# Channel attention: products of channels by pairs of image columns on two column halves of TensorE, and strip-edge rows in 64x32 tiles with two edges at once

## The chip, the cores and the metric

The kernel runs on one core of one Trainium2 chip. The metric is the device time of one launch in microseconds (us), the median of several runs. The five engines of the core are called TensorE (PE; its weight loads PEld), VectorE (DVE), ScalarE (ACT), GpSimd (POOL) and SyncE (SP). SP and ACT also issue DMA transfers, each on its own queue (SPq, ACTq).

## The reference

Two layers on an input of 4 images, 192 channels and 128 by 128 pixels, in f32. The change touches the first, a channel attention with 8 heads of 24 channels:

```
qkv = dwconv3x3(conv1x1(x, w_qkv), w_dw)          # 768 channels
q, k, v, l = jnp.split(qkv, 4, axis=1)
q = q / jnp.maximum(jnp.linalg.norm(q, axis=-1, keepdims=True), EPS)   # over the 16384 pixels
k = k / jnp.maximum(jnp.linalg.norm(k, axis=-1, keepdims=True), EPS)
attn = jnp.einsum('bhcn,bhdn->bhcd', q, k) * temperature[None]         # 24 x 24 per head and image
attn = jax.nn.softmax(attn, axis=-1)
out = jnp.einsum('bhcd,bhdn->bhcn', attn, v).reshape(b, c, h, w)
...
out = conv1x1(L + out + x, w_proj) + L
```

L is a gate made from the mean of l. The second layer is a dilated local attention on the result. For the change it matters that each head needs, for every image, the 24 by 24 products of the convolved q and k channels over all pixels, and the squared norms of these channels.

## The kernel before, in words

The kernel has three parts in a row. The first pass (to about 845 us) makes the 1x1 products for q, k and v, convolves v, and writes q and k unconvolved into a DRAM buffer, `qk_dram`, ordered by image row, channel, image and column. `channel_attention` (about 845 to 1560 us) reads them back, convolves them on TensorE, and makes the attention weights and from these a mixing matrix for each image. The second pass (to the end) applies it and does the second layer. The first and last part have written-out plans; in `channel_attention` only the order of TensorE is that of the program text, and a scheduler places the instructions of the other engines, the DMA issues on SP and ACT among them.

A head is worked in two stages. In the **convolution**, `head` walks over its 48 channels (24 of q, then 24 of k). An image's 128 rows are cut into four strips of 32 rows, and a channel's four strips lie on the four groups of 32 partitions. `loaded` brings eight channels at a time: 16 transfers on SP's queue (L717) into one of three buffers (`lent`, and two called `u`), and one small transfer `few` (L703), from which POOL builds `band`, the matrices that apply the vertical taps (L728, L730). `convolve` (L738) multiplies with three of these, one for each horizontal tap, as 32 by 32 tiles: a strip sees only its own rows. `evicted` copies the sums from PSUM on ACT (L747) into one large tile for q and one for k, and VectorE takes the statistics for the norms (L749, `bn_stats`). These large tiles are ordered by image, group of four columns, channel and column in the group, so that four columns of all 24 channels are 96 adjacent numbers.

In the **products** (`products`), TensorE multiplies for each image and each group of four columns the 96 numbers of q with the 96 of k over the 128 rows (L838), and sums over the 32 groups into `gram`; of the result only the places with equal column count, which `kept` and `part` pick out at the end (L850, L856).

Rows at the inner edges of the strips are missing from this: for each of the three edges, two rows on either side. `cut_loaded` (L776) brings the four rows of the head's 24 channels, once for q and once for k, 96 partitions each; `cut_taps` (L766) brings the taps as a matrix. `cut_convolved` (L786) multiplies them, three taps by q and k, into `pcut`, q in the lower half of the partitions and k in the upper; ACT copies `pcut` to `s_cut` (L798), TensorE turns `s_cut` (L804) so that pixels lie on partitions, ACT copies that to `cutT` (L806), VectorE squares it and adds the squares to the norms (L811, L814). Small matmuls (L834) make the products of the edges, in the middle of the last image.

The order of TensorE in `products` is: for image 0, 1 and 2 the edge convolution of edge 0, 1 or 2, the 32 matmuls of the image, the turning of that edge; then image 3; then the folding of the sums (L858 to L866). Edge 0's rows are loaded by SP ahead of time, edges 1 and 2 by ACT's queue after the edge convolution that frees the buffers: there is one buffer for q and one for k. In images 0 and 1 the second half of the image's matmuls is preceded by the matmuls of the previous head's mixing matrix (`mix`, L906), with weights `wph` that were loaded once for all heads. The next head's rows (`lent`, `u`) are loaded by SP while the products run, as buffers come free. The softmax of a head (`finish`) and the gate are spread over the next head's convolution.

In the built program every DMA carries one of eight completion semaphores, taken in turn over both queues, and waits for the transfer that had this semaphore before it.

Of the kernel before, what the change touches and what calls it, by code (L numbers as in the profile page):

```python
# [670 lines left out]
def channel_attention(tc, d, load, qk_dram, mix1, mix2, band_p, u_p, gate_p, lent, gates):  # L671
# [7 lines left out]
    with ExitStack() as ctx:  # L679
# [11 lines left out]
        for band in bands:  # L691
            nc.gpsimd.memset(band, 0.0)
        logits = fin.tile([CH0, B, 2, CH0], F32, tag="logits", name="logits")
# [52 lines left out]
        def evicted(full, stats, ch, pc):  # L746
            nc.scalar.copy(full[:, :, :, ch, :], pc.rearrange("p b (v w) -> p b v w", w=4))  # L747
            for b in range(B):
                nc.vector.bn_stats(stats[:, b, ch, :], full[:, b, :, ch, :])  # L749
# [12 lines left out]
        def cut_taps(hd):  # L762
            both = []
            for which in range(2):
                t = cut_p.tile([4 * CH0, 3, 2 * CH0], F32, tag=f"taps{which}", name=f"cuttaps{which}_{hd}")
                nc.sync.dma_start(t, d["cuttaps"][:, which * HEADS0 + hd])  # L766
                both.append(t)
            return both

        def cut_loaded(hd, edge, queue):  # L770
            us = []
            for which in range(2):
                c0 = which * C + hd * CH0
                u = cut_p.tile([4 * CH0, B * W], F32, tag=f"u{which}", name=f"cut{which}_{hd}_{edge}")
                first = (edge + 1) * STRIP - 2
                queue.dma_start(u, qk_dram[first : first + 4, c0 : c0 + CH0].rearrange("r c b w -> r c (b w)"))  # L776
                us.append(u)
            return us

        def cut_convolved(hd, edge, us, taps):  # L780

            pcut = ps_c.tile([128, B, W], F32, tag="pc", name=f"pcut{hd}_{edge}")
            for dx in (1, 0, 2):
                to, of = shifted(dx)
                for which in range(2):
                    nc.tensor.matmul(  # L786
                        pcut[which * G : which * G + 2 * CH0, :, to],
                        taps[which][:, dx, :],
                        us[which].rearrange("p (b w) -> p b w", w=W)[:, :, of],
                        start=dx == 1,  # L790
                        stop=dx == 2,
                    )
            s_cut = cut_p.tile([128, B, W], F32, tag="s_cut", name=f"s_cut{hd}_{edge}")
            if hd == 0 and edge == 0:
                nc.gpsimd.memset(s_cut, 0.0)
            for which in range(2):
                rows = slice(which * G, which * G + 2 * CH0)
                nc.scalar.copy(s_cut[rows], pcut[rows])  # L798
            return s_cut

        def cut_turned(hd, edge, s_cut):
# [4 lines left out]
            nc.scalar.copy(cut, turned.rearrange("p b (k c) -> p b k c", k=2)[:, :, :, : 2 * CH0])  # L806
            return cut

        def cut_squares(hd, edge, cut, sums):
            square = st.tile([128, B, 2, 2 * CH0], F32, tag="square", name=f"square{hd}_{edge}")  # L810
            nc.vector.tensor_mul(square, cut, cut)  # L811
            for which, sq in enumerate(sums):
                for r in range(2):
                    nc.vector.tensor_add(sq, sq, square[:, :, which, r * CH0 : (r + 1) * CH0])  # L814

        def products(hd, q, sq, k, sk, us, taps):
            gram = ps_c.tile([128, B, W], F32, tag="pc", name=f"gram{hd}")[:HALF, :, :HALF]
            cuts, two = [], 2 * CH0
            for b in range(B):
                if b < 3:  # L820
                    s_cut = cut_convolved(hd, b, us, taps)
                    if b < 2:
                        us = cut_loaded(hd, b + 1, nc.scalar)
                for v in range(W // 4):
# [12 lines left out]
                    four = lambda a: a[:, b, v].rearrange("p c w -> p (c w)")  # L837
                    nc.tensor.matmul(gram[:, b, :], four(q), four(k), start=v == 0, stop=v == W // 4 - 1)  # L838
# [3 lines left out]

            own = st.tile([two, B, CH0], F32, tag="own", name=f"own{hd}")
            other = st.tile([two, B, CH0], F32, tag="other", name=f"other{hd}")
            for r, to in enumerate((own, other)):
                pick_row = same_row[:, r : r + 1].unsqueeze(1).to_broadcast([two, B, CH0])
                nc.vector.tensor_mul(to, extra[:, :, r * CH0 : (r + 1) * CH0], pick_row)
            nc.vector.tensor_add(own, own, other)
            kept = st.tile([128, B, CH0, 4], F32, tag="square", name=f"kept{hd}")[:HALF]
            nc.vector.tensor_mul(  # L850
                kept,
                gram.rearrange("p b (c w) -> p b c w", w=4),
                same.unsqueeze(1).unsqueeze(1).to_broadcast([HALF, B, CH0, 4]),
            )
            part = st.tile([HALF, B * CH0], F32, tag="part", name=f"part{hd}")
            nc.vector.reduce_sum(part, kept.rearrange("p b c w -> p (b c) w"), axis=AX.X)  # L856
# [17 lines left out]
        def finish(hd):  # L874
# [21 lines left out]
            mixes.append(mix(hd))  # L896

        def mix(hd):

            low = min(max(128 - hd * CH0, 0), CH0)  # L900
            for b in range(0, B, 2):
# [3 lines left out]
                for e in range(2):  # L905
                    nc.tensor.matmul(two[:, e, :], logits[:, b + e, hd % 2, :], wph[:, hd, :], start=True, stop=True)  # L906
# [18 lines left out]
        def head(hd):  # L925

            fulls, stats = [], []
            for which, pool in enumerate((q_p, k_p)):
                fulls.append(pool.tile([128, B, W // 4, CH0, 4], F32, tag="conv", name=f"conv{which}_{hd}"))
# [3 lines left out]
            for _, n, dx in order:  # L933
                which, j, e = n // CH0, n % CH0 // 4, n % 4
                if dx == 1:
                    if n % 8 == 0:
                        sources[n // 8] = loaded(hd, which, j)
                    if n == 40:
                        taps = cut_taps(hd)
                        us = cut_loaded(hd, 0, nc.sync)  # L940
# [12 lines left out]
        same, same_row, fold, fold_rows, ones, ident, wph, tempr = (  # L953
            load(wts, n) for n in "same same_row fold fold_rows ones ident wph temp".split()
# [517 lines left out]
def _shapes_only():  # L1472
# [4 lines left out]
    eye = np.eye(C, dtype=f).reshape(2, HALF, C).transpose(1, 0, 2)  # L1477
    pick = np.zeros((128, QR + 32), f)
# [123 lines left out]
```

## Time and profile before

| | us |
|---|---|
| median of 3 runs | 4336.97 (4332.42 to 4344.78) |
| the profiled execution, device time | 4341.44 |
| its span, first to last instruction | 4339.7 |
| TensorE busy over the span | 4154.4 (96%) |
| VectorE busy | 3816.2 (88%) |
| POOL busy | 3395.5 (78%) |
| ACT busy | 2633.3 (61%) |
| channel attention alone, 845 to 1560 us: TensorE busy | 673.8 of 715 |
| VectorE / ACT / POOL busy there | 419.6 / 285.3 / 206.0 |
| L838 gram, busy on TensorE | 192.6 |
| L786 edge convolution, busy on TensorE | 90.7, idle before it 28.0 |
| L738 convolution, busy on TensorE | 262.9 (rows from `u`), 140.0 (from `lent`) |

Busy time of TensorE is the union of its instructions, which overlap. A timeline line gives start, duration, engine, source line, operation, the tile written and the tiles read, the shape (stationary, then moving operand), the number of instructions merged, and in brackets the idle time before with what ended it. An f32 matmul stands as two records. A line of windows gives for each engine the busy time and the number of instructions, then the granted clock of TensorE as a share, the busy share of the DMA engines and the GB/s moved.

### The profile page before, as it was taken

The page shows a single profiled execution, that of the slowest core. Times are in us where ns is not written, and L with a number is a line of the kernel's source. Part 1 is how long each engine was busy: PE and PEld are TensorE (multiplying, and loading weights), DVE is VectorE, ACT ScalarE, POOL GpSimd, SP SyncE. Part 2 cuts the span into 40 slices and gives each one's busy share as a digit, 9 for nine tenths or more (in the row PEclk, how much of TensorE's full clock was granted, in tenths as well). Part 3 has the DMA queues.
Part 4 walks back from the last instruction along what each step waited for, and adds up shares of the span by engine and source line. Part 5 has one row for each costly group of instructions (what it writes and reads, how often), then busy time and mean ns, then how long its engine had stood idle before and what let it go on. Part 6 is the DMA issues. An engine that isn't in the chain of part 4 may idle for free.

```text
span 4339.7 us, 74888 instructions
## 1 busy us (share of the span) xinstructions
PE 4154.4 (96%) x25728; PEld 1722.2 (40%) x25728; DVE 3816.2 (88%) x5572; ACT 2633.3 (61%) x4906; POOL 3395.5 (78%) x3411
## 2 busy tenths in 40 slices
PE   8999999798999988999999999999999999999996
PEld 3333333376666632333333333333333333333331
DVE  6999999865566637999999999999999999999996
ACT  6999999743344456556566555665656556566531
POOL 6888888732233115999999999999999999999998
PEclk9999999899999999999999999999999999999997
DMA  7888898666556657566665566655556555655521
GB/s 236 265 267 256 266 287 279 202 184 171 162 148 178 169 123 138 122 133 124 135 131 128 131 121 133 136 119 131 125 132 133 129 130 124 136 133 126 115 51 32
DMA packets 483019, 676.93 MB, mean 156 GB/s; under 512 B 142848, under 2 KB 318412, under 8 KB 482640
## 3 DMA queue, kind: packets, MB, share of 16 engines
q1 hardware_dynamic: 440352, 498.53, 41.1%
q0 software_dynamic: 37888, 166.74, 20.9%
q10 hardware_dynamic: 4400, 6.88, 0.5%
q8 instruction: 204, 3.34, 0.3%
q14 instruction: 175, 1.43, 0.1%
HBM read 278.18 MB, written 201.33 MB: 110 GB/s over the span
## 4 chain that ended last, share of the span: by engine, by line
PE 72%; DVE 13%; DMA 4%; issue 4%; POOL 4%; ACT 1%; SPq 1%; POOLq 0%; DVEq 0%; ACTq 0%
PE sc L1260 9%; PE ex L1382 8%; PE ph L1027 7%; PE pu L427 7%; PE pc L738 6%; PE pkv L1181 5%; DVE term L1388 4%; PE pkv L1184 4%; PE pu L432 3%; PE q L1241 3%; PE gram L838 3%; PE q L1238 3%; POOL acc L1391 3%; DVE prod L1249 3%; PE pu L578 2%
## 5 line engine op out<-in xcount | busy, mean ns | idle before, releaser
L1391 POOL TENSOR_TENSOR acc<-acc,term 128x512 f32<-128x512 f32 x1536 | 2034.6, 1330 | 145.3 <-DVE term L1388 58.9
L1388 DVE TENSOR_TENSOR term<-ex,vring 128x512 f32<-128x512 f32 (+2 forms) x1596 | 1000.1, 663 | 56.1 <-PE ex L1382 42.6
L1249 DVE TENSOR_TENSOR prod<-q,kring 128x1536 f32<-128x1536 f32 (+1 forms) x600 | 1007.4, 1688 | 23.6 <-PE q L1238 9.0
L504 POOL TENSOR_TENSOR v_True<-v_True,side 128x512 f32<-128x512 f32 (+1 forms) x512 | 643.1, 1268 | 127.7 <-ACT side L493 98.4
L1382 PE MATMUL ex<-e_sb,spread 108*128 108x512 bf16 x1728 | 568.0, 387 | 55.6 <-DVE term L1388 31.8
L481 DVE SCALAR_TENSOR_TENSOR pa<-vboth,dwv,pa 128x1024 f32<-128x1024 f32 (+1 forms) x448 | 574.3, 1282 | 44.3 <-ACT pa L474 14.5
L1194 ACT COPY kring<-pkv 64x512 f32<-64x512 f32 x384 | 223.2, 581 | 416.0 <-PE pkv L1184 410.5
L1079 DVE SCALAR_TENSOR_TENSOR pa<-hboth,posw,pa 128x1024 f32<-128x1024 f32 (+1 forms) x320 | 408.3, 1276 | 35.9 <-ACT pa L1067 16.9
L1260 PE MATMUL sc<-prod,pick 128*32 128x512 f32 x3456 | 429.0, 598 | 1.8 <-DVE prod L1249 1.8
L728 POOL COPY band<-few 32x720 f32<-32x720 f32 x192 | 150.6, 784 | 335.9 <-DMA few<-in_bands 289.8
L1382 PEld LDWEIGHTS <-spread 108*128 108x128 bf16 x1728 | 133.3, 98 | 666.8 <-issue 640.9
L1407 ACT COPY o<-po 128x512 f32<-128x512 f32 x192 | 106.2, 588 | 447.2 <-PE po L1404 241.9
L427 PE MATMUL pu<-xt,wx 128*128 128x512 f32 x768 | 360.5, 613 | 17.1 <-ACT vboth L463 8.7
L1027 PE MATMUL ph<-lent,mix 128*64 128x512 f32 (+1 forms) x1024 | 373.7, 595 | 0.5 <-DMA mix<-mixed 0.5
L1181 PE MATMUL pkv<-y,wkv 128*128 128x512 f32 x768 | 364.3, 596 | 9.2 <-DMA y<-moved 9.0
L493 ACT ACTIVATE side<-ring,dwv 128x512 f32<-128x512 f32 (+1 forms) x512 | 347.9, 724 | 30.5 <-POOL v_True L504 26.5
L1111 ACT ACTIVATE side<-hring,posw 128x512 f32<-128x512 f32 (+1 forms) x512 | 340.9, 710 | 16.7 <-DMA side<-side 14.8
L749 DVE BATCH_NORM_STATS2 stats<-conv 128x6 f32<-128x128 f32 x1536 | 301.5, 271 | 17.0 <-ACT conv L747 15.3
L747 ACT COPY conv<-pc 128x512 f32<-128x512 f32 x384 | 219.1, 585 | 123.5 <-PE pc L738 116.4
L738 PE MATMUL pc<-u,band 32*32 32x508 f32 (+1 forms) x6144 | 262.9, 595 | 2.4 <-DMA u<-qk_dram 2.3
L1194 ACT COPY vring<-pkv 64x512 f32<-64x512 f32 x384 | 223.9, 583 | 45.6 <-PE pkv L1184 32.2
L427 PEld LDWEIGHTS pu<-xt,wx 128*128 128x128 f32 x768 | 143.6, 194 | 224.4 <-issue 124.2
(170 smaller groups left out, 6489.2 us busy)
## 6 DMA issues: line engine op xcount, KB each, us to landing
qk_dram<-us SPq DMA_DIRECT2D x192, 512.0 KB
side<-side POOLq DMA_DIRECT2D x124, 768.0 KB, 7.2
u<-qk_dram SPq DMA_DIRECT2D x512, 128.0 KB
xt<-in_x SPq DMA_DIRECT2D x64, 512.0 KB
v_dram<-v_False SPq DMA_DIRECT2D x64, 512.0 KB
lent<-qk_dram SPq DMA_DIRECT2D x256, 128.0 KB
lent<-in_x SPq DMA_DIRECT2D x128, 256.0 KB
lent<-v_dram SPq DMA_DIRECT2D x128, 256.0 KB
```

Source lines behind the costliest of these rows:

```text
L427: mm(pu, wx[:, mt * 128 : (mt + 1) * 128], tiles["xt", n][:, im, :], start=True, stop=False)
L481: nc.vector.scalar_tensor_tensor(by_row(to[:, o : o + length]), by_row(vboth[:, at : at + length, :, t % 3 : t % 3 + W]), dwv[:, 0, t : t ...
L504: nc.gpsimd.tensor_add(v[:, rows, :], v[:, rows, :], z[:, rows, :])
L738: nc.tensor.matmul(pc[r * STRIP : (r + 1) * STRIP, :, to], band[at, e, c, dx, :], u[at, e, c, :].rearrange("p (b w) -> p b w", w=W)[:, :, of],
L1027: mm(to, w[:, cols], tiles["xv", n, j, im], start=j == 0, stop=j == 2)
L1181: mm(rows3(tile_of("pc", key)), w, tiles["y", n, im], start=True, stop=False)
L1194: nc.scalar.copy(rows[HALVES[im], :, pad : pad + W], rows3(tiles["pkv", n, pair, im])[HALVES[e]])
L1249: nc.vector.tensor_mul(to[:, :, px].rearrange("p t (r w) -> p t r w", w=W), q.unsqueeze(1).to_broadcast([128, 3, *q.shape[1:]]), three,)
L1260: mm(sc[quad * 32 : (quad + 1) * 32, :], pick[:, QR - 4 * row : QR - 4 * row + 32], tiles["prod", n, k // NT, k % NT // 3][:, k % 3, :], s ...
L1382: mm(rows3(tile_of("ex", ("ex", n, g, t))), spread[:, t, :], e_sb, start=True, stop=True)
L1388: nc.vector.tensor_mul(rows3(to[:, px]), rows3(ex[:, px]), win)
L1391: nc.gpsimd.tensor_add(tiles["acc", n, g], tiles["acc", n, g], tiles.pop(("term", n, g, t)))
```

## The change

The large tiles of q and k are ordered by image, **pair** of columns, channel and column in the pair. For each image there are 64 pairs; a matmul takes 48 numbers of q and 48 of k, and successive pairs go to the lower and the upper half of the output partitions, that is, of TensorE's columns. `kept` and `part` are made for each half.

Edge rows: the 24 channels are split into two halves of 12. A half's four rows lie on 48 partitions of the lower or the upper 64, and q and k side by side in one buffer; so an edge has four transfers (L775 in the new text) instead of two, half as large. The taps come as one tile. `cut_convolved` takes a list of edges and multiplies in tiles of 64 rows by 32 columns; edges 0 and 1 are done together at the start of the products, on eight tiles, edge 2 alone at the end of image 0, on four. There are two buffers: edges 0 and 1 are loaded by SP with the head's last rows, edge 2 by ACT's queue after edges 0 and 1 are convolved. `cut_kept` is the copy to `s_cut`, now one instruction an edge. In odd edges the halves lie the other way round, which the copy to `cutT` undoes. The squares and the picking of rows follow the new order. `wph` is loaded for each head anew, on ACT's queue, when its softmax is done. The tables of constants (`same`, `same_row`, `fold`, `fold_rows`, `cuttaps`) are laid out to match.

```diff
-            nc.scalar.copy(full[:, :, :, ch, :], pc.rearrange("p b (v w) -> p b v w", w=4))
+            nc.scalar.copy(full[:, :, :, ch, :], pc.rearrange("p b (v w) -> p b v w", w=2))
...
         def cut_taps(hd):
+            taps = cut_p.tile([128, 2, 3, STRIP], F32, tag="taps", name=f"cuttaps{hd}")
+            nc.sync.dma_start(taps, d["cuttaps"][:, hd])
+            return taps
+
+        def cut_loaded(hd, edge, queue):
+            u = cut_p.tile([128, 2, B * W], F32, tag=f"u{edge % 2}", name=f"cut{hd}_{edge}")
+            first = (edge + 1) * STRIP - 2
             for which in range(2):
+                for h in range(2):
+                    c0 = which * C + hd * CH0 + h * (CH0 // 2)
+                    queue.dma_start(
+                        u[h * G : h * G + 2 * CH0, which],
+                        qk_dram[first : first + 4, c0 : c0 + CH0 // 2].rearrange("r c b w -> r c (b w)"),
+                    )
+            return u
+
+        def cut_convolved(hd, edges, us, taps):
+
+            pcut = {edge: ps_c.tile([128, B, W], F32, tag="pc", name=f"pcut{hd}_{edge}") for edge in edges}
             for dx in (1, 0, 2):
                 to, of = shifted(dx)
+                for edge in edges:
+                    for which in range(2):
+                        for h in range(2):
+                            rows = slice(h * G, h * G + 2 * CH0)
+                            at = (2 * which + (h + edge) % 2) * STRIP
+                            nc.tensor.matmul(
+                                pcut[edge][at : at + STRIP, :, to],
+                                taps[rows, which, dx, :],
+                                us[edge][rows, which].rearrange("p (b w) -> p b w", w=W)[:, :, of],
+                                start=dx == 1,
+                                stop=dx == 2,
+                            )
+            return pcut
+
+        def cut_kept(hd, edge, pcut):
             s_cut = cut_p.tile([128, B, W], F32, tag="s_cut", name=f"s_cut{hd}_{edge}")
-            if hd == 0 and edge == 0:
-                nc.gpsimd.memset(s_cut, 0.0)
-            for which in range(2):
-                rows = slice(which * G, which * G + 2 * CH0)
-                nc.scalar.copy(s_cut[rows], pcut[rows])
+            nc.scalar.copy(s_cut, pcut[edge])
             return s_cut
...
         def products(hd, q, sq, k, sk, us, taps):
-            gram = ps_c.tile([128, B, W], F32, tag="pc", name=f"gram{hd}")[:HALF, :, :HALF]
+            gram = ps_c.tile([128, B, W], F32, tag="pc", name=f"gram{hd}")[:, :, : 2 * CH0]
             cuts, two = [], 2 * CH0
+            pcut = cut_convolved(hd, (0, 1), us, taps)
+            us[2] = cut_loaded(hd, 2, nc.scalar)
+            s_cut = cut_kept(hd, 0, pcut)
             for b in range(B):
-                if b < 3:
-                    s_cut = cut_convolved(hd, b, us, taps)
-                    if b < 2:
-                        us = cut_loaded(hd, b + 1, nc.scalar)
...
-                    four = lambda a: a[:, b, v].rearrange("p c w -> p (c w)")
-                    nc.tensor.matmul(gram[:, b, :], four(q), four(k), start=v == 0, stop=v == W // 4 - 1)
+                    for e in range(2):
+                        pair = lambda a: a[:, b, 2 * v + e].rearrange("p c w -> p (c w)")
+                        nc.tensor.matmul(
+                            gram[e * G : e * G + two, b, :], pair(q), pair(k), start=v == 0, stop=v == W // 4 - 1
+                        )
                 if b < 3:
                     cuts.append(cut_turned(hd, b, s_cut))
                     cut_squares(hd, b, cuts[b], (sq, sk))
-
+                if b == 0:
+                    pcut.update(cut_convolved(hd, (2,), us, taps))
+                if b < 2:
+                    s_cut = cut_kept(hd, b + 1, pcut)
...
+            kept = st.tile([128, B, CH0, 2], F32, tag="kept", name=f"kept{hd}")
+            for e in range(2):
+                rows = slice(e * G, e * G + two)
+                nc.vector.tensor_mul(
+                    kept[rows],
+                    gram[rows].rearrange("p b (c w) -> p b c w", w=2),
+                    same[rows].unsqueeze(1).unsqueeze(1).to_broadcast([two, B, CH0, 2]),
+                )
+                nc.vector.reduce_sum(part[rows], kept[rows].rearrange("p b c w -> p (b c) w"), axis=AX.X)
...
         def mix(hd):

             low = min(max(128 - hd * CH0, 0), CH0)
+            wph = fin.tile([CH0, C], F32, tag="wph", name=f"wph{hd}")
+            nc.scalar.dma_start(wph, d["wph"][:, hd, :])
+            yield
...
-                fulls.append(pool.tile([128, B, W // 4, CH0, 4], F32, tag="conv", name=f"conv{which}_{hd}"))
+                fulls.append(pool.tile([128, B, W // 2, CH0, 2], F32, tag="conv", name=f"conv{which}_{hd}"))
...
                         taps = cut_taps(hd)
-                        us = cut_loaded(hd, 0, nc.sync)
+                        us = {edge: cut_loaded(hd, edge, nc.sync) for edge in range(2)}
```

## The prediction

> **What bounds the kernel now.** I read the page first, then the channel attention alone (845 to 1560 us) by waits, then each head cut into its convolution and its products, then one head's timeline by engine. The products of head 2 and of head 7, and the convolution before head 2's products, by windows:
>
> ```profile
> core 0: us, PE busy (x) PEld busy (x) DVE busy (x) ACT busy (x) POOL busy (x), PEclk, DMA share, GB/s
> 1066.30:1114.00 47.70, 42.53 (x359) 30.53 (x364) 11.89 (x39) 7.14 (x12) 13.01 (x36) 0.86 0.53 142
> ...
> 1510.20:1547.60 37.40, 37.21 (x354) 28.83 (x353) 10.70 (x39) 7.13 (x12) 0.00 (x0) 1.00 0.08 25
> ```
>
> ```profile
> 1024.60:1066.30 41.70, 41.66 (x1154) 30.38 (x1154) 40.44 (x201) 28.40 (x51) 13.94 (x36) 1.00 0.73 192
> ```
>
> In the products TensorE carries the time and all else is idle; in the convolution VectorE is busy for 40.4 of 41.7 us, so that stage yields nothing to a faster TensorE. The eight product stretches are 37.6, 46.9, 47.7, 45.6, 46.3, 46.3, 44.1 and 37.4 us (351.9). Heads 1 to 6 take some 9 us more than 0 and 7; TensorE's timeline in head 2 shows where:
>
> ```profile
> 1066.26 2.77 PE L786 MATMUL pcut<-cut,cuttaps 96*48 96x512 f32 x12
> ...
> 1072.60 2.96 PE L838 MATMUL gram<-conv,conv 128*96 128x96 f32 x32
> ...
> 1078.27 1.91 PE L786 MATMUL pcut<-cut,cuttaps 96*48 96x512 f32 x2 [2.28 <-DMA cut<-qk_dram]
> 1082.31 5.33 PE L786 MATMUL pcut<-cut,cuttaps 96*48 96x512 f32 x10 [2.12 <-DMA cut<-qk_dram]
> 1087.57 4.95 PE L838 MATMUL gram<-conv,conv 128*96 128x96 f32 x32
> ...
> 1099.23 5.68 PE L838 MATMUL gram<-conv,conv 128*96 128x96 f32 x64
> ...
> 1107.99 1.28 PE L834 MATMUL sm<-cutT 128*48 128x48 f32 x24
> ```
>
> Edge 1's rows come late, and what follows runs slow: ten edge records take 5.33 us where twelve took 2.77, and 32 gram records 4.95 instead of 2.96, with a granted clock of 0.86 in this stretch against 1.00 in head 7. A matmul has two records. The loads, in ScalarE's and SyncE's timelines of the same head and SyncE's waits over the stage:
>
> ```profile
> 1072.67 0.66 ACTq L776 DMA_DIRECT2D cut<-qk_dram  x1
> ```
>
> ```profile
> 1059.04 9.29 SPq L717 DMA_DIRECT2D lent<-qk_dram  x16
> ```
>
> ```profile
> SPq L717 <- DMA cut<-qk_dram: 75.7, 21, 7.1
> ```
>
> ScalarE issues edge 1's two loads at 1071.58 and 1072.67, 5.3 and 6.4 us after the products begin, and the second lands at 1082.3, 9.6 us after its issue. SyncE begins the next head's rows 7.2 us before the products. They share the DMA with the next head's rows, and in the built program each transfer also waits for the one that used its completion semaphore (of eight, in turn) before it, across both queues.
>
> **The change, part by part.** T is the start of a head's products. Times are against the profiled execution: span 4339.7, device 4341.4, which is 4.5 above the median of the runs.
>
> Gram. Before: 1024 matmuls of 96 by 96, 64 records an image, 5.68 us, so (5.68-0.25)/64 = 85 ns a record. After: twice as many of 48 by 48, alternating between two halves of the columns. A record of that shape stands in the trace in one half only (L834): (1.28-0.21)/24 = 45 ns. That the halves run beside each other is bounded by: 45 ns a record (no overlap) and 22.5 (full). The nearest rows are the edge records, two tiles of 64 columns over the same rows: twelve in 2.77 us, where one alone takes 0.59 and follows its own tile's last by 0.43, that is six rounds of two, full overlap. I take 24 ns: 3.1 us an image.
>
> [...]
>
> Edge convolution. Before: three edges of 2.77 us, each on two tiles. After: edges 0 and 1 together on eight tiles, 48 records in six rounds of 0.43: 2.8 us; edge 2 on four tiles, 24 records, also 2.8 at full clock. Two thirds of the old time. The convolution at L738 runs on 16 such diagonal tiles into one bank.
>
> Loads. Edges 0 and 1 now come on SP's queue behind the last group of the head's own rows: 7.2 us before T, where the next head's rows begin now, eight transfers and one for the taps instead of two and two. So edge 1's wait goes. **Late next are edge 2 and s_cut of edge 0.** Edge 2's four transfers are issued by ScalarE after pcut of edges 0 and 1, and s_cut's copy stands behind all four in ScalarE's order; turned of edge 0 on TensorE waits for that copy, and behind it edge 2's convolution and images 1 to 3. Before, the first of two issues fell 5.3 to 6.3 us after T. The semaphore that the first now needs belongs to a transfer four places earlier (2.3 us), but SP's queue runs some 4.5 us later (nine transfers at 0.3 to 0.65): T+8 for the first, T+11 for the fourth, whose semaphore belongs to the second transfer of the next group. s_cut is done at T+11.6, edge 2 (same bytes as edge 1 before, which took 8 to 11 us from first issue to last landing) at T+17.3. TensorE has done pcut and image 0 by 2.8+3.1+0.8 = 6.7. So it idles, and the clock falls as in head 2.
>
> One head of 1 to 6: 17.3, edge 2 at the slow clock 5.3, image 1 partly slow 4.1, pm 0.8, turned 0.5, image 2 3.1, turned 0.5, image 3 3.1, extra products 1.15, tail 1.9 (as now): 37.7 against 46.1 on average, 8.4 saved, 50 for six. Head 0: its first issue came 2.8 us after T with nothing ahead of it, the landing 10.7 after T; full clock: 10.7+2.8+3.1+0.5+3.1+0.5+3.1+1.15+1.9 = 27, saves 10.6. Head 7 has no next head's rows: landing T+8.7 (issues at 2.8 to 5.2 as head 7's were, and an estimate of 3.5 to land), 25.7, saves 11.7. Together 72.
>
> Taken off: the edges' rows land behind the last group, 0 to 1 us after the convolution's end; and the built order sends each group's bands (few) just before its rows, where some went earlier; POOL needs 4.7 us for a group's copies (4 of 784 ns, 8 of 196) and by my estimate of SP's queue has 2 us in hand. I take 1 us for each of seven heads, 7; the ends are 0 and 5 each (0 and 35).
>
> Everything else goes on covered engines. ScalarE: 24 s_cut copies fewer (0.58 each, 14 us) and one wph load a head; it is busy 7 of 47 us in the products. wph for the last head is placed by the built order in head 7's products, so its tail hides it; without that it costs one load, under 6 us (an edge load of head 7, issued at 1513.86, was in use at 1519.83). VectorE: kept and part in two halves instead of one, about 1.1 us either way, on the path in the tail. The sums at L814 and the reversed read at cutT keep size and count. SP's later next group delays nothing: it needs 62 us of queue a head (96 row transfers at 0.57, few, edges), the shorter period is 80.
>
> The convolution's copy now writes runs of two instead of four, and bn_stats reads them. ScalarE's 585 ns for runs of four equals 588 (L1407) for contiguous ones, and it has 13 us a head in hand. VectorE has none:
>
> ```profile
> L749 DVE BATCH_NORM_STATS2 stats<-conv 128x6 f32<-128x128 f32 x1536 | 301.5, 271 | 17.0 <-ACT conv L747 15.3
> ...
> L758 DVE TENSOR_TENSOR sq<-sq,stats 128x96 f32<-128x96 f32 x16 | 5.4, 336 | 0.6
> ...
> L757 DVE TENSOR_SCALAR sq<-sq 128x96 f32<-128x96 f32 x16 | 3.8, 240 | 0.6
> ```
>
> bn_stats is free of cost at one end, since runs of four leave it at 301.5/1536 = 196 ns for 128 elements. The other end is a read that hops at every element, (336-240)/96 = 1 ns an element, 128 ns an instruction, 197 us in all. A gain has no ground: the elements are as many. I take 0: a run of two is nearer to the run of four. [...] No row here has pairs.
>
> Sum: 4341.4 - 72 + 7 = 4276, at the median's level **4271**.
>
> **The rivals.** *The edge comes earlier*: if edge 2 lands at T+13, the gap is short enough for the clock to hold (head 0 kept it through 1.8 us), a head takes 13+2.8+14.15 = 30: 47 us more saved, 4224. For it: fewer of SP's transfers may stand ahead. Against: 8 to 11 us a load in every busy head. *The convolution loses*: 4 us a head from late bands or rows, 21 more than taken: 4292. VectorE's 95% speaks for it, the 2 us in hand against. *The halves don't overlap*: 45 ns a record adds 2.7 us to images 1 to 3, 8 a head, 65: 4336, no change. The edge records speak against it. *Slower*: VectorE's read of pairs costs. It decides at 66/1536 = 43 ns an instruction (a third of the hopping price), and at the full price gives 4468; the rest of the change can't pay it, since the convolution has no slack on VectorE. Against it: runs of four are free.
>
> **How the numbers follow.** Likeliest case 0.54 (own range 4240 to 4300: landing 3 us either way over six heads, the convolution's 0 to 3), earlier edge 0.10, convolution loses 0.14, halves don't overlap 0.10, slower 0.12. Faster by over 0.3% (13 us, about what a measurement of this kernel tells from none): the first three, 0.78; within: 0.10; slower: 0.12. The range 4215 to 4340 holds all but the last and the edge of the second.
>
> **What would show it.** Gram's busy time near 100 us instead of 192.6; edge records 5.6 us a head; TensorE in heads 1 to 6 waiting for s_cut some 5 us and for edge 2 some 5, with a clock below 1 in those stretches; product stretches near 38, 27 and 26 us; convolutions still 42 to 43 with VectorE at 40 and bn_stats at 196 ns. Wrong if bn_stats grows, if gram stays near 180 us, or if edge 2 lands after T+25.

## The result, and the profile after

The changed kernel takes 4292.48 us (median of 4 runs, 4289.94 to 4295.9), 0.9896 of the time before (95% interval 0.9878 to 0.9913): 45 us faster, where 66 were forecast. The profiled executions differ by more than the medians: span 4339.7 before, 4288.2 after, 51.5 less. Of these, 59.5 come from the products and 14.1 are lost in the convolutions of heads 1 to 7. The rest nearly cancels inside the channel attention (its chain of heads ends at 1501.2 us instead of 1547.6), and 5 us lie behind it.

The windows of the eight product stretches after the change, with the columns as before (busy time and number for each engine, then the granted clock, the DMA share, GB/s):

```profile
896.70:928.76 32.06, 29.28 (x643) 18.96 (x650) 11.79 (x39) 4.99 (x9) 12.92 (x36) 0.84 0.51 140
972.80:1015.39 42.59, 34.86 (x652) 19.88 (x657) 11.63 (x42) 5.27 (x9) 13.06 (x36) 0.80 0.57 157
1058.80:1101.91 43.11, 39.66 (x652) 23.75 (x657) 13.05 (x42) 5.27 (x9) 13.52 (x36) 0.72 0.58 159
1145.85:1182.13 36.28, 33.32 (x651) 19.94 (x657) 11.52 (x42) 5.23 (x9) 10.80 (x30) 0.86 0.59 167
1226.56:1262.23 35.67, 33.33 (x652) 20.64 (x657) 11.65 (x42) 5.26 (x9) 10.14 (x28) 0.81 0.60 165
1306.47:1341.17 34.70, 32.80 (x652) 20.59 (x657) 11.56 (x42) 5.27 (x9) 8.49 (x24) 0.80 0.56 156
1386.29:1417.47 31.18, 28.40 (x652) 17.88 (x656) 11.10 (x42) 5.28 (x9) 8.39 (x24) 1.00 0.52 149
1464.40:1501.22 36.82, 34.60 (x647) 21.08 (x645) 11.05 (x42) 5.26 (x9) 0.00 (x0) 0.81 0.30 79
```

Only head 6 has the clock at 1.00. In head 2 TensorE shows as busy for 39.66 of 43.11 us, but much of that runs at half speed (a granted clock of 0.50 from 1064.4 to 1074.7 us and from 1078.9 to 1087.0). Its timeline there (the last line is image 3's first half, at a granted clock of 1.00):

```profile
1058.80 1.43 PE L791 MATMUL pcut<-cut,cuttaps 48*32 48x512 f32 x10
1060.39 1.04 PE L791 MATMUL pcut<-cut,cuttaps 48*32 48x512 f32 x2 [0.16 <-DMA cut<-qk_dram]
1062.20 5.19 PE L791 MATMUL pcut<-cut,cuttaps 48*32 48x512 f32 x36 [0.77 <-DMA cut<-qk_dram]
1067.32 2.80 PE L847 MATMUL gram<-conv,conv 128*48 128x48 f32 x64
...
1078.89 5.30 PE L791 MATMUL pcut<-cut,cuttaps 48*32 48x512 f32 x18 [0.56 <-DMA cut<-qk_dram]
1084.12 2.80 PE L847 MATMUL gram<-conv,conv 128*48 128x48 f32 x64
...
1091.92 3.09 PE L847 MATMUL gram<-conv,conv 128*48 128x48 f32 x128
...
1095.52 1.64 PE L847 MATMUL gram<-conv,conv 128*48 128x48 f32 x64
```

Edges 0 and 1 (L791), 2.8 us of work (2.79 in head 0), last from 1058.80 to 1067.3, because their rows trickle in; the clock then falls (granted 1.00 up to 1064.4, 0.50 from there to 1074.7), and half an image takes 2.80 us where the last line has 1.64. What brought the rows, in SyncE's and ScalarE's timelines of the same head:

```profile
1051.08 5.14 SPq L775 DMA_DIRECT2D cut<-qk_dram  x8
1056.33 0.42 SPq L705 DMA_DIRECT2D few<-in_bands  x1
1056.85 12.12 SPq L719 DMA_DIRECT2D lent<-qk_dram  x16
```

```profile
1069.41 3.18 ACTq L775 DMA_DIRECT2D cut<-qk_dram  x4
1072.63 0.58 ACT L802 COPY s_cut<-pcut 128x512 f32<-128x512 f32 x1 [12.85 <-DMA few<-in_bands]
```

The eight edge transfers take 5.14 us to issue, up to 1056.22, 2.6 us before the stretch begins. TensorE's weight loads show the last wait for their rows:

```profile
1063.23 0.18 PEld L791 LDWEIGHTS pcut<-cut,cuttaps 48*32 48x32 f32 x16 [0.90 <-DMA cut<-qk_dram]
```

It ends 4.4 us into the stretch and seven us after the last issue. Edge 2's four issues follow 10.6 us after the start of the stretch, and s_cut's copy stands behind them.

The convolution: the windows of heads 1, 2 (the shortest) and 7 (the longest), then the two groups whose operands became runs of two columns (busy time, mean of one in ns, idle time before and what ended most of it), and ScalarE's copy as it was before:

```profile
928.76:972.80 44.04, 44.04 (x1152) 29.87 (x1153) 40.93 (x201) 29.71 (x51) 8.86 (x24) 1.00 0.66 176
1015.39:1058.80 43.41, 42.68 (x1152) 29.01 (x1152) 40.62 (x201) 29.57 (x51) 12.86 (x36) 1.00 0.66 179
...
1417.47:1464.40 46.93, 45.90 (x1154) 26.98 (x1153) 42.25 (x201) 29.22 (x51) 17.24 (x48) 1.00 0.80 208
```

```profile
L751 DVE BATCH_NORM_STATS2 stats<-conv 128x6 f32<-128x128 f32 x1536 | 304.4, 274 | 29.2 <-ACT conv L749 26.6
L749 ACT COPY conv<-pc 128x512 f32<-128x512 f32 x384 | 228.7, 616 | 127.6 <-PE pc L740 120.5
```

```profile
L747 ACT COPY conv<-pc 128x512 f32<-128x512 f32 x384 | 219.1, 585 | 123.5 <-PE pc L738 116.4 <-POOL band L730 3.3
```

VectorE is still the bound there (40.2 to 42.3 us busy over the seven heads), bn_stats rose from 271 to 274 ns, and its idle time behind ScalarE from 15.3 to 26.6 us. ScalarE's copy rose from 585 to 616 ns.

### The profile page after: what moved, and what is told of

It reads as the page before. It is cut to its first block, busy times and chain, and to the rows that moved or that the text cites. A ratio compares the mean times of both kernels' runs of the same rounds, so it can differ in the third digit from the quotient of the medians.

```text
span 4288.2 us, 79574 instructions
## 1 busy us (share of the span) xinstructions
PE 4115.1 (96%) x28064; PEld 1642.4 (38%) x28064; DVE 3820.6 (89%) x5588; ACT 2627.7 (61%) x4882; POOL 3388.9 (79%) x3411
## 4 chain that ended last, share of the span: by engine, by line
PE 68%; DVE 14%; DMA 5%; issue 4%; POOL 3%; SPq 3%; ACT 1%; ACTq 0%; POOLq 0%; DVEq 0%
PE sc L1281 9%; PE ex L1403 8%; PE ph L1048 7%; PE pu L427 6%; PE pkv L1202 5%; PE pc L740 5%; DVE term L1409 4%; PE pkv L1205 4%; PE q L1262 4%; PE q L1259 4%; PE pu L432 3%; DVE prod L1270 3%; PE gram L847 2%; POOL acc L1412 2%; SPq L719 2%
## 5 line engine op out<-in xcount | busy, mean ns | idle before, releaser
L481 DVE SCALAR_TENSOR_TENSOR pa<-vboth,dwv,pa 128x1024 f32<-128x1024 f32 (+1 forms) x448 | 574.2, 1282 | 42.2 <-ACT pa L474 14.4
L1100 DVE SCALAR_TENSOR_TENSOR pa<-hboth,posw,pa 128x1024 f32<-128x1024 f32 (+1 forms) x320 | 407.5, 1273 | 37.0 <-ACT pa L1088 18.1
L751 DVE BATCH_NORM_STATS2 stats<-conv 128x6 f32<-128x128 f32 x1536 | 304.4, 274 | 29.2 <-ACT conv L749 26.6
L749 ACT COPY conv<-pc 128x512 f32<-128x512 f32 x384 | 228.7, 616 | 127.6 <-PE pc L740 120.5
L740 PE MATMUL pc<-u,band 32*32 32x508 f32 (+1 forms) x6144 | 276.0, 595 | 4.1 <-DMA u<-qk_dram 1.9
```

The lines of the kernel that those rows point to most:

```text
L481: nc.vector.scalar_tensor_tensor(by_row(to[:, o : o + length]), by_row(vboth[:, at : at + length, :, t % 3 : t % 3 + W]), dwv[:, 0, t : t ...
L740: nc.tensor.matmul(pc[r * STRIP : (r + 1) * STRIP, :, to], band[at, e, c, dx, :], u[at, e, c, :].rearrange("p (b w) -> p b w", w=W)[:, :, of],
```

## The experiments

Every run stands beside runs of the kernel before on the same chip (medians 4334.8 to 4339.3). "Products" is the sum of the eight product stretches, "convolution" that of heads 1 to 7, both from the profiled execution; where a stretch ends can be read to some hundredths of a us, so the sums may be off by 0.2. Head 0's convolution is in neither sum: 54.0 us before, 55 to 56 in most runs, 60 to 64 in the five from "three buffers, ACT" to the last "one half". What follows the heads is the same program everywhere and took 2781 to 2798 us in these executions, so the time of one execution says little about differences below some 15 us; the medians and the two sums say more.

| kernel | us | ratio to before (95%) | products | convolution |
|---|---|---|---|---|
| before | 4337.36 | 1 | 352.0 | 297.8 |
| changed | 4292.48 | 0.9896 (0.9878 to 0.9913) | 292.5 | 311.9 |
| gram alone | 4319.32 | 0.9952 (0.9937 to 0.9967) | 329.3 | 305.2 |
| edges alone | 4327.15 | 0.9967 (0.9955 to 0.9980) | 333.9 | 308.8 |
| pairs in one half | 4327.15 | 0.9970 (0.9959 to 0.9981) | 334.7 | 304.1 |
| edges 0, 1 early | 4278.75 | 0.9854 (0.9825 to 0.9883) | 246.3 | 345.4 |
| three buffers, SP | 4251.67 | 0.9797 (0.9783 to 0.9812) | 194.8 | 374.2 |
| the same, later | 4271.46 | 0.9846 (0.9823 to 0.9868) | 193.7 | 393.2 |
| three buffers, ACT | 4244.56 | 0.9787 (0.9753 to 0.9821) | 246.9 | 306.2 |
| the same, fours | 4288.45 | 0.9875 (0.9854 to 0.9897) | 286.3 | 307.1 |
| ACT in written order | 4270.82 | 0.9843 (0.9826 to 0.9861) | 193.7 | 377.0 |
| the same, fours | 4342.55 | 1.0007 (0.9997 to 1.0017) | 270.5 | 372.5 |
| the same, one half | 4352.71 | 1.0029 (1.0017 to 1.0041) | 279.7 | 372.7 |
| an issue each third copy | 4275.95 | 0.9870 (0.9851 to 0.9889) | 202.3 | 378.5 |

The theory at the start: the gram and the edge records cost what was forecast, and what is missing went into late rows of edges 0 and 1 and into the convolution. The rivals: the halves overlap only in part, or the ScalarE chain (four issues, s_cut, edge 2) takes the time as forecast.

### One part at a time

Gram by pairs, with the edges' rows, tiles and order as before:

```diff
-            pcut = cut_convolved(hd, (0, 1), us, taps)
-            us[2] = cut_loaded(hd, 2, nc.scalar)
...
+                if b < 3:
+                    s_cut = cut_convolved(hd, b, us, taps)
+                    if b < 2:
+                        us = cut_loaded(hd, b + 1, nc.scalar)
...
```

> The gram by pairs on two halves, the edges as in the kernel before. An image of 64 pairs should take 3.1 us instead of 5.68 (that the halves overlap). In heads 0 and 7 all four images count, 10 us a head; in heads 1 to 6 image 0 only lengthens the wait for edge 1, so three count, 7.8 us. Together about 67 us less than before (4337), less what the convolution loses. Theory A, that the convolution's 1.6 us a head come from the copy into runs of two (619 ns instead of 585, 48 a head): convolutions of 44, in all 4283. Theory B, that they come from the order of the loads: convolutions of 42.5, in all 4270.

It gave 20 us, and both theories missed by more than they differ. An image takes 3.1 us instead of 5.68 (124 of its 128 records 3.04), but the stretches shortened by 22.7 in all, since the time went into the edges' chain. TensorE in head 3:

```profile
1161.36 1.11 PE L806 MATMUL turned<-ident,s_cut 128*128 128x128 f32 x4 [3.43 <-ACT s_cut L800]
1165.83 1.91 PE L788 MATMUL pcut<-cut,cuttaps 96*48 96x512 f32 x2 [3.35 <-DMA cut<-qk_dram]
1170.01 3.63 PE L788 MATMUL pcut<-cut,cuttaps 96*48 96x512 f32 x8 [2.27 <-DMA cut<-qk_dram]
```

Three waits, nine us together, stand in that stretch, and eight edge records then take 3.63 us, where twelve took 2.77 in the kernel before: with a shorter image TensorE only comes earlier to what it waits for.

The edge rows, tiles and loading of the change, with the gram by fours:

```diff
-            nc.scalar.copy(full[:, :, :, ch, :], pc.rearrange("p b (v w) -> p b v w", w=2))
+            nc.scalar.copy(full[:, :, :, ch, :], pc.rearrange("p b (v w) -> p b v w", w=4))
...
+                    four = lambda a: a[:, b, v].rearrange("p c w -> p (c w)")
+                    nc.tensor.matmul(gram[:, b, :], four(q), four(k), start=v == 0, stop=v == W // 4 - 1)
...
```

> The edges as in the changed kernel, the gram by four columns in one piece as before. Edge convolution 5.6 us a head instead of 8.3, 22 us in all; the wait for edge 1 (9 us in six heads) gone, the waits for edges 0 and 1 and for edge 2 of the changed kernel in its place, of which each image's longer gram hides 2.6 us more. Products 44 us a head as before: 4325 to 4345 in all. Theory A: convolutions of 42.5 us. Theory B: 44.

4327.15 lies in the range, but by other terms: the products fell to 41.7 us a head where 44 were expected, 18.1 in all, and the convolution lost 11.0. The gram alone lost it 7.4, so both parts slow the convolution, and neither alone explains the 14.1. Alone the two parts give 20 and 12 us, together 45: each is worth more beside the other.

### Do the two halves of the columns run beside each other?

```diff
-                            gram[e * G : e * G + two, b, :], pair(q), pair(k), start=v == 0, stop=v == W // 4 - 1
+                            gram[:two, b, :], pair(q), pair(k), start=v + e == 0, stop=v + e == W // 4
...
-            for e in range(2):
+            for e in range(1):
```

> The changed kernel with all pairs of columns summed in the lower half of the output partitions; the upper half of the folding is left at zero. The same number of records of the same shape on one half of the columns. If the halves overlap in the changed kernel, a record takes 45 ns here and an image 5.8 us, 2.7 us more each; image 0 of most heads partly hides it: 8 to 11 us a head, 4355 to 4375 against 4292. If the gain came from the shorter weight load or the smaller shape alone, 4292 as it is.

It is 35 us slower than the change. TensorE's timeline shows an image:

```profile
1093.77 5.96 PE L847 MATMUL gram<-conv,conv 128*48 128x48 f32 x128
```

46.6 ns a record (5.96 over 128) against 24 (3.08) with the halves in turn: the halves overlap almost completely. The time moved by less than expected, 5.3 us a head where 11.5 more are computed, because longer images lie beside late rows again.

### Edges 0 and 1 earlier

```diff
-                    if n == 40:
+                    if n == 8:
                         taps = cut_taps(hd)
                         us = {edge: cut_loaded(hd, edge, nc.sync) for edge in range(2)}
```

> The rows of edges 0 and 1 are loaded with the second group of the head instead of the sixth; nothing else moves. Theory X, the waits add up in a chain: the two edges start with the product stretch, but then ScalarE's four issues and the rows of edge 2 are waited for as first forecast, so a stretch stays near 36 us (292.5 us over eight heads in the changed kernel) and the time is 4285 to 4300. Theory Y, the late rows of edges 0 and 1 cost 42 us over seven heads by themselves: the stretches sum to some 250, and the time is 4245 to 4255, less what the convolution loses to the four-row transfers taking their turn earlier (up to 2 us a head).

Theory Y holds for the products, which fall by 46.2; the time, 4278.75, fell by 14 only and lies between the two. Edges 0 and 1 now take 2.79 us in every head (TensorE, head 3):

```profile
1137.81 2.79 PE L791 MATMUL pcut<-cut,cuttaps 48*32 48x512 f32 x48
```

ScalarE's first issue now falls 2.8 us after the start of the stretch in all heads but one, s_cut is done at 6.1 to 7.8 and image 1 starts at 12.4 to 19.3, on average over heads 1 to 6 at 14.9. In heads 1 to 7 of the changed kernel the first two are 5.0 to 11.0 and 8.3 to 14.8, and image 1 of heads 1 to 6 starts at 21.9 on average. So the late rows of edges 0 and 1 add about seven us to the chain behind edge 2. The convolution lost 33.5 us more than in the change: with the same transfers, only placed ahead of the head's other rows.

### All three edges ahead

Three buffers, and twelve transfers on SP's queue with the head's second group (`kept` shares the buffer of `square` to make room):

```diff
-            u = cut_p.tile([128, 2, B * W], F32, tag=f"u{edge % 2}", name=f"cut{hd}_{edge}")
+            u = cut_p.tile([128, 2, B * W], F32, tag=f"u{edge}", name=f"cut{hd}_{edge}")
...
-            us[2] = cut_loaded(hd, 2, nc.scalar)
...
-                    if n == 40:
+                    if n == 8:
                         taps = cut_taps(hd)
-                        us = {edge: cut_loaded(hd, edge, nc.sync) for edge in range(2)}
+                        us = {edge: cut_loaded(hd, edge, nc.sync) for edge in range(3)}
```

> The changed kernel with a buffer for each of the three edges, all twelve transfers and the taps issued by SP with the second group of the head's rows instead of the last, none by ScalarE. If the late edge rows and the slow clock after them are what is left in the products: no wait in them, 25.5 us a head (2.8 edges, 3.1 an image, 0.7 a turning, 2.8 edge 2, the rest as now) instead of 36.5, 88 us less in all, 4205. Rival, that the DMA then is the bound: SP needs 62 us of queue a head, the period would be 69; if the convolution then waits for rows it grows to 47 to 50 us and the time stays above 4230.

Every stretch is 23.0 to 24.8 us, at full clock (1.00 granted in all eight). But the rival came true as well: the convolution takes 53 us, and 62 of 98 us won in the products are given back. TensorE's waits from 950 us on (waiter, what it waited for, us in total, times, longest) name the rows and the bands; the second pair is the changed kernel's:

```profile
PEld pc L740 <- DMA u<-qk_dram: 37.4, 93, 1.1
PEld pc L740 <- POOL band L732: 36.8, 30, 4.0
```

```profile
PEld pc L740 <- DMA u<-qk_dram: 27.8, 63, 1.7
PEld pc L740 <- POOL band L732: 8.2, 9, 1.4
```

The bands grew most. Waits for rows in `lent` add 14.4 us (14.8 after 0.4).

With the same issue in the fourth group (`n == 24`):

> As the kernel with three edge buffers, but the twelve transfers go out with the fourth group of the head and not with the second. If SP's queue is simply full (70 us of issues and stalls a head), the convolution keeps its 53 us and the time stays at 4245 to 4260. If the order was the cause (the bands of the next group behind 7.8 us of edge issues while that group's rows are needed soonest), the convolution falls back to about 45 and the time to 4200.

The convolution got worse, 56 us: two groups later doesn't help, and the bands, which stand behind the twelve in SP's order, are now what is late most:

```profile
PEld pc L740 <- POOL band L732: 78.7, 20, 10.9
```

### The transfers off SP's queue

Three buffers, one transfer on ScalarE's queue behind each eviction of channels 8 to 19 (`cut_loaded` now hands out its four transfers one at a time):

```diff
...
+                        us, ahead = {}, []
+                        for edge in range(3):
+                            us[edge], parts = cut_loaded(hd, edge, nc.scalar)
+                            ahead.append(parts)
...
                 evicted(fulls[which], stats[which], e * (CH0 // 4) + j, pcs.pop(n))
+                if n >= 8:
+                    for parts in ahead:
+                        if next(parts, 0) is None:
+                            break
```

> Three edge buffers, and the twelve transfers issued on ScalarE's queue, one behind each eviction of channels 8 to 19; SP's queue carries none of them. If the time of SP's queue bounded the kernel with three buffers, the convolution takes 43 to 45 us, the products 24.4 as there, and the time is 4280 less 97 with the products' sum at 195 in place of 292: about 4190. If it was the transfers themselves (DMA engines), the convolution stays above 50 and the time near 4250. If ScalarE becomes the bound (48 evictions of 0.615 and 12 issues of 0.65, 37 us of a convolution of 43), the convolution is 46 to 48 and the time about 4215.

The convolution is back at 44 us without the twelve transfers. That it was SP's queue that bounded it, and not the transfers as such, this run alone doesn't show: as built, all twelve go out during the products, so the convolution has none. The next section has them in the convolution again, on ScalarE's queue. The products did not stay at 24.4, and ScalarE's timeline in head 2 (its queue's issues among its copies) shows why:

```profile
1052.01 4.97 ACTq L776 DMA_DIRECT2D cut<-qk_dram  x5
1057.07 2.15 ACTq L932 DMA_DIRECT2D mix<-mixed  x2
1060.51 0.65 ACTq L776 DMA_DIRECT2D cut<-qk_dram  x1
1061.21 0.48 ACT L813 COPY cutT<-turned 128x384 f32<-128x384 f32 x1 [11.64 <-DMA mix<-mixed]
```

In the built order the next head's transfers are not spread over its evictions; they stand between the edges of this head's products. ScalarE does no other work for 11.6 us, and cutT, whose turned edge was ready at 1053.4, starts at 1061.2. It is still the fastest kernel of all, level with the three buffers on SP within the intervals: 93 us under the kernel before.

The same with the gram by fours:

> The same loading ahead on ScalarE's queue, with the gram by fours of columns as in the kernel before. If the gram is then the only thing left in a stretch, each of four images takes 5.7 us instead of 3.1, a stretch 35 instead of 24.4, and the time lies 75 to 85 us above the pairs with the same loading, less some 8 for the copy into runs of four: about 4260. If pairs are worth no more than what they gave alone (18 us against the kernel before), the two lie within 30 us.

44 us slower (4288.45 against 4244.56), between the two expectations. That here too the longer gram fills time in which the chain is waited for fits this, and was not tested by itself.

### ScalarE in the written order

```diff
-        with tc.manual_schedule(engines={mybir.EngineType.PE}):
+        with tc.manual_schedule(engines={mybir.EngineType.PE, mybir.EngineType.Activation}):
```

> As the edges' transfers spread over ScalarE's evictions, with ScalarE's instructions kept in the written order: the transfers of the next head no longer go out between the transposed edges of this one. If those issues were all that lengthened its product stretches (31.4 to 34.6 us in heads 1 to 6), the products fall to 24.4 us a head as with three buffers on SP's queue, 195 in all, the convolution keeps 43 to 44, and the time falls by 52 to about 4193. If issue and eviction then hinder each other in the convolution, it rises to 46 a head and the time is about 4215.

The products are 24.4 us a head in heads 1 to 6, at full clock in the one shown below (1.00): with the issues gone from them nothing of their lengthening is left (the written order moved ScalarE's other instructions too). The convolution went to 54, above both expectations. The same twelve transfers stand in it as with three buffers on SP's queue, but TensorE now waits for ScalarE's copies (87.2 us from 950 us on, where the changed kernel has 2.2), hardly more for rows in `u` (32.7 after 27.8), and bands are not among its waits. So at this pace of 54 us it is the place in SP's queue, and not the transfers as such, that makes bands and rows late. Whether another queue could carry them through a convolution of 44 us no run shows. Two variants share this loading and differ in the gram alone, so that its price can be read with nothing late. The gram by fours, and all pairs in one half:

> The same with the gram by fours of columns. An image is 5.68 us there against 3.08, so with nothing late in a stretch it takes 24.4 and four times 2.6, 34.8; the convolution gains up to 1 us a head from the shorter copy. The time is 75 to 83 us above the pairs with the same order, about 4270. If the gram's longer images only fill time in which the edges' chain is waited for, the two differ by less than 45, as 4288 and 4245 did without the written order.

> The same with all pairs in one half of the columns. An image took 5.96 us in the kernel that changed this alone, 2.88 more than on two halves: with nothing late in a stretch that is 11.5 a head, 92 in all, so the time is about 4285, somewhat above the fours. If a part stays hidden as it did there (5.3 us a head), the time is near 4235.

One stretch of each (windows of pairs on two halves, fours, pairs on one half):

```profile
1059.24:1083.63 24.39, 23.23 (x652) 17.18 (x657) 11.60 (x42) 3.99 (x8) 8.95 (x24) 1.00 0.74 204
```

```profile
1078.43:1112.39 33.96, 33.18 (x396) 27.36 (x400) 10.95 (x39) 3.99 (x8) 12.60 (x36) 1.00 0.60 164
```

```profile
1083.67:1118.76 35.09, 34.72 (x652) 28.67 (x657) 11.04 (x40) 3.99 (x8) 12.59 (x36) 1.00 0.59 153
```

The pairs save 9.6 us a head against the fours, 72 us in time (4342.55 less 4270.82), slightly under the expected difference (the absolute numbers expected stood on 4193); on one half they save nothing. With nothing late this is the price of the gram part, and all of it comes from the second half of the columns. The fours with these loads are a lesson by themselves: 81.5 us were taken out of the products and the time stayed at 1.0007, since the convolutions gave 75 back, and head 0's another 8 (62.5 us instead of 54.0).

Last, one issue behind every third eviction (`if n >= 8 and n % 3 == 2`), to test whether the 0.65 us of each issue lengthened the convolution:

> ScalarE's instructions in the written order as before, but a transfer behind every third eviction (channels 8, 11, ... 41) instead of behind each of twelve in a row. In the run with the written order the twelve took 1172.5 to 1192.5 us, 1.66 us a channel where the other channels take some 0.9, each issue 0.62 to 0.66 and waiting besides for an earlier transfer: 12 times 0.76 is 9 of the 10 us that its convolution lost. If so, an issue in three evictions hides (0.62 + 0.22 < 0.9) and the convolution is 44 to 46, the products stay at 24.4, and the time is 4271 less 7 times 8.5, about 4210. If each issue costs its 0.65 us wherever it stands, the convolution stays at 51 to 54 and the time above 4250.

That theory falls: the convolution stayed at 54. ScalarE's timeline in head 4's convolution, and one of TensorE's and one of ScalarE's waits from 950 us on, and TensorE's in the changed kernel:

```profile
1179.58 1.64 ACT L749 COPY conv<-pc 128x512 f32<-128x512 f32 x3 [0.41 <-PE pc L740]
1185.76 0.62 ACTq L776 DMA_DIRECT2D cut<-qk_dram  x1
1186.43 1.61 ACT L749 COPY conv<-pc 128x512 f32<-128x512 f32 x3 [5.21 <-DMA u<-qk_dram]
```

```profile
PEld pc L740 <- ACT conv L749: 96.7, 92, 4.3
ACT conv L749 <- DMA u<-qk_dram: 77.7, 22, 5.4
```

```profile
PEld pc L740 <- ACT conv L749: 2.2, 5, 0.7
```

The issue is not long, it is late: ScalarE stands still from 1181.2 to 1185.8 in front of it, and the evictions stand behind. The trace has what it waits for: the completion semaphore that it uses itself, and that a row transfer of SP's, issued at 1179.95, had before it. That transfer lands at 1185.74, 0.02 us before the issue starts. Of the 82 edge issues in this kernel's seven convolutions, 47 begin so, within 0.1 us of the landing that frees their semaphore, 44 of them behind rows of SP's queue; ScalarE stands idle for 94 us in front of them, and the convolutions are 66.6 us longer than in the change. With the twelve in a row it was 49 of 84 and 43 us, 29 of them behind an earlier edge transfer of ScalarE's own. So that the issues wait for the eight semaphores is shown. That this is the whole loss is not: no run changed the number of semaphores, or had ScalarE in the written order without these transfers.

## Why the prediction was right or wrong

**Right.** The gram's record: 24 ns taken, 3.08 us an image measured at a granted clock of 1.00, here and in the kernels with edges 0 and 1 early, with three buffers on SP's queue and with ScalarE in the written order; on one half of the columns a record took 46.6 ns. The edge records: 2.79 us for edges 0 and 1, 2.77 for edge 2, when their rows are there. bn_stats on pairs: 0 taken, 2.9 us of 301.5 measured (274 ns an instruction against 271), so the rival on the other side had no ground. That the products of heads 1 to 6 would run with a clock below 1: five of six do (0.72 to 0.86), and it costs where it wasn't counted: the gram's busy time is 119.6 us instead of the 100 that would show it, through half images at 2.80 us.

**Wrong: "the edges' rows land behind the last group, 0 to 1 us after the convolution's end".** From the start of a stretch to the first gram record took 5.7, 8.5, 10.9, 10.4, 9.4, 5.7 and 10.9 us in heads 1 to 7 instead of 2.8, in sum 42 us more, in a term for which 7 was taken. Of the 42, 31 are rows that come late (the last edge matmuls to get theirs begin 3.0 to 5.9 us after the start), and 11 the half clock (0.50 granted) under which the rest of the records then run in heads 2 to 5 and 7 (1.05 us a record instead of 0.59). The estimate had counted the rows from their issue and not through their landing: the last were in use only seven us after the last issue in head 2, with the next head's rows right behind them.

**Right number, wrong cause: 37.7 us for heads 1 to 6.** They took 37.3 on average. But it was meant as edges on time, then ScalarE's issue at 8 us and edge 2 at 17.3. What happened is that the late edges 0 and 1 pushed everything behind them: a wait for s_cut of 5 us stands only in head 1, TensorE's idle times before edge 2's records are 0.93 us at most where some 5 were expected, and image 1 began at 21.9 us on average where 22.6 was implied. With the first edges on time it began at 14.9, and the same heads took 30.8. So the chain behind edge 2 had been put 7 us too late, and the late edges made up for it. That the sum came out right was luck.

**Wrong sizes: heads 0 and 7.** 32.1 and 36.8 us against 27 and 25.7. Head 7 was taken as free of competition, having no next head's rows; its edges 0 and 1 came as late as any (10.9 us to the first gram record), with the second pass's rows following them on SP's queue from 1462.40 us on. Head 0 waited for edge 2: image 1 began at 16.6 us where 13.5 was implied (10.7 and 2.8).

**Undersized: the convolution.** Seven us were taken for it together with the late edges; it lost 14.1. Its rival said 4 us a head and 4292, which is the measured time, but the loss was 2 a head: that it names the right number is a coincidence of the two terms. Gram alone and edges alone lost 7.4 and 11.0. The copy's 31 ns more were costed at nothing for ScalarE's slack; VectorE's idle time behind that copy rose by 11.3 us over the kernel, but not for the copy's length: with the gram alone, which has the longer copy, it is 15.1 us, as before, and with the edges alone, which has the old one (586 ns), 23.7. What made the gram alone lose its 7.4 us stays open.

The sum closes: products forecast at 27 + 6 x 37.7 + 25.7 = 278.9, measured 292.5, 13.6 more; convolution 14.1 for 7, 7.1 more; 66 less 20.7 is 45.3, and the heads' sequence ended 46.4 us sooner. In the medians the saving is 45.

## What to carry to other kernels

In this stage, a chain of short matmuls fed by late transfers, a faster matmul first turned into waiting: the same gram change was worth 20 us beside the old edge loads and 72 with all rows there. Look for the wait that the longer work covered, and price a load to its landing and not to its issue. Moving transfers ahead wasn't free either: on SP's queue the convolutions gave back 62 of the 98 us won in the products, and on ScalarE's in the written order, one behind every third copy, 47 of 82 issues began within 0.1 us of the landing that freed their semaphore, and the convolutions were 66.6 us longer than in the change. So sum both stages before you claim the gain.

## What the runs showed of the hardware that was not expected

Two column halves of TensorE with the same rows overlapped almost completely in f32 at 48 columns: 24 ns a record, against 46.6 with all pairs on one half. Waits of under a microsecond went with a lost clock: in head 2 two waits of 0.16 and 0.77 us, with few edge records between them, stand before records at half speed, and the half images that start at 1067.32 and 1071.45 us still take 2.80 us instead of 1.64; the granted clock there is 0.50 from 1064.4 to 1074.7 us. An edge transfer half as large (48 rows of 2 KB) took as long to issue as a whole one did: 5.14 us for 8, 0.64 each, where two of 96 rows took 1.30. ScalarE's copy from PSUM took 616 ns when it wrote runs of two, 585 with runs of four.
